# A state-space layer on one core: tokens on partitions for the norm, sums taken by ScalarE, and B replicated from fp32 rows

## The chip, the cores and the metric

The kernel runs on one core of a Trainium2 chip. A core has a matrix engine (PE, with its weight loads listed apart as PEld), a vector engine (DVE), a scalar engine (ACT), a general engine (POOL) and a sync engine (SP), which here issues all DMAs. Each runs its own list of instructions in order and waits for the others through semaphores. SBUF holds the working tiles, PSUM the outputs of PE. The metric is the device time in microseconds of one execution, and a time is the median of several runs.

## The reference

The network has four layers on x of shape (4, 96, 64, 64). The change lies in the first one alone: two Mamba blocks with residuals over sequences of 4096 tokens and 96 channels, a global pool, a 1x1 fusion and a batch norm over all tokens. Cut to what matters:

```python
def _mamba_block(seq, ...):                     # twice, for each of 4 batches
    mu = seq.mean(-1, keepdims=True)
    var = ((seq - mu) ** 2).mean(-1, keepdims=True)
    h = (seq - mu) * rsqrt(var + EPS) * ln_g + ln_b
    xs, z = split(h @ in_w)                     # 192 channels each
    xc = silu(causal_conv4(xs) + conv_b)
    dt, Bm, Cm = split(xc @ xproj_w)            # 6, 16, 16
    delta = softplus(dt @ dt_w + dt_b)
    dA = exp(delta[..., None] * A)              # 192 x 16 states
    dBx = delta[..., None] * Bm[:, :, None, :] * xc[..., None]
    hstates = scan(h = dA * h_prev + dBx)       # along the tokens
    y = einsum('blds,bls->bld', hstates, Cm) + Dp * xc
    return (y * silu(z)) @ out_w
...
out = fus_w @ concat([mamba_out, relu(pool(x) @ gp_w.T + gp_b)]) + fus_b
out = (out - out.mean((0, 2, 3))) * rsqrt(out.var((0, 2, 3)) + EPS) * bn_g + bn_b
return out + x
```

## The kernel before

Layer 0 cuts the 4096 tokens of a batch into 4 chunks of T = 1024. An item is one chunk of one batch in one of the two blocks, so there are 32 items, in the order chunk, block (i = 0 or 1), batch. The 192 x 16 = 3072 states of an item are 24 tiles of 128 partitions (32 channels times 4 states) by 1024 tokens.

For each tile m (24 to an item) the kernel does this:

- `rep` (from L191's helper `mm`, L195): PE multiplies a 0/1 matrix `sel_b` with rows that hold B, so that each of the four states' B is replicated over 32 partitions; the result `x` fills two banks of PSUM. One rep serves the tiles of a group (nine groups in an item, starting at tiles 0, 3, 6, 8, 11, 14, 16, 19 and 22).
- `exp` (L455): ACT computes dA as `exp(nega * delta)` from `ddb`, a copy of delta replicated through DRAM. For most tiles it goes to SBUF (`da`) three tiles ahead. For the eight tiles 2, 5, 7, 10, 13, 15, 18 and 21 it goes to PSUM (`dap`) one tile ahead, into the buffers that rep's `x` and `u` also use.
- `scan`: DVE multiplies `udb` (delta times xc, replicated) by rep's `x` into `u` in PSUM (L471), then scans (L475). For the eight tiles named above POOL has computed the product (`times_b`, L461, `up`), and DVE only scans.
- `times_c` (L481): POOL multiplies the states by C (`crep`); `sum_y` (L500): PE adds the states up into `y`; `gate` (L511): DVE multiplies by silu(z).

Everything else of an item is its first stage, spread over slots of tiles of the item before: a step marked `at_slot(t)` of item k is issued at tile 24 k + t - 24. Its steps are: load x (slot -11), `center` product that takes the mean off (-7), Square and a copy to `n` on ACT (-6), sum of squares by a product with ones (-5), Ln and Exp on ACT (-4), the scaling of `n` on DVE (-3, L299), the products with the conv taps `w_x` (-2 to 1), Silu, the product `xproj` that gives B, C (three times over) and dt (slot 5), and then delta and z. `project` (slot 39 of the item itself, 15 of the next) and `finish` (41) make the output `x`, and `keep_stats` (42, L537) takes batch statistics of it for i = 1.

B is replicated in bfloat16 as three parts that add up to the fp32 value: ACT casts the first 32 rows of the projection to `r3` (L335), PE subtracts that part from the other rows with the matrix `part` (`less`, L342), ACT casts again (`next_part`, L347), twice; rep then contracts over 96 rows.

`with tc.manual_schedule(...)` fixes the order on PE, DVE, ACT and POOL as it is written: within a tile, scan, rep or exp for the next tiles, times_c, keep_state, times_b, then the sums, project and finish, and last the first-stage steps of the items that follow. Only two one-bank buffers (`tile_ps`, tag `ps`) serve all first-stage products and project, so a step often waits for the eviction of an earlier one.

Of the kernel before, what the change touches and what calls it, by code (L numbers as in the profile page):

```python
# [50 lines left out]
class Net:  # L51
# [20 lines left out]
    def consts(self, ctx):  # L72
# [15 lines left out]
        self.stats = pool.tile([C, NT // MB, 6], F32, name="stats")  # L88
# [4 lines left out]
    def layer0(self, dram, scratch):  # L93
        tc, nc, ins = self.tc, self.nc, self.ins
        x_in = ins["x"]
        with ExitStack() as ctx:
# [19 lines left out]
            sel_b = cp.tile([C, 4, 128], BF16, name="sel_bq")  # L116
            part = cp.tile([C, 2, C], BF16, name="partq")
            fo = cp.tile([128, 3, C], F32, name="fo")
            dp = cp.tile([128, 2, 3, 128], F32, name="dp")
            sel_r = load(cp, "sel_r", [128, 32])  # L120
            xproj = load(cp, "xproj", [128, 3, 2, 3 * 2 * NST + DTR])
# [7 lines left out]
            fbias = cp.tile([C, B], F32, name="fbias")  # L129
            pooled = cp.tile([C, B * NSC], F32, name="pooled")  # L130

            with tc.tile_pool(name="l0s", bufs=1) as wk:
# [30 lines left out]
                nc.vector.tensor_copy(sel_b, load(wk, "sel_b", [C, 4, 128]))  # L163
                nc.vector.tensor_copy(part, load(wk, "part", [C, 2, C]))
# [14 lines left out]
            dbl = cp.tile([97 + DTR, T], F32, name="dbl")  # L179
            nc.vector.memset(dbl[C:], 1.0)  # L180
            r3s = [cp.tile([C, T], BF16, name=f"r3{k}") for k in range(2)]
            for r3 in r3s:
                nc.vector.memset(r3, 0.0)
# [7 lines left out]

            def mm(ps, w, rhs, start=True, stop=True, shift=0, **kw):
                for at in halves:
                    at_in = slice(at.start + shift, at.stop + shift)
                    nc.tensor.matmul(ps[:, at], w, rhs[:, at_in], start=start, stop=stop, **kw)  # L195
# [54 lines left out]
            def first_stage(k):  # L250
# [11 lines left out]
                @at_slot(-11)  # L262
                def _():
                    m["xn"] = load_x(b, s, i)
                    if s == 0:
                        nc.gpsimd.memset(n[:, :3], 0.0)
                    else:
                        nc.gpsimd.tensor_copy(n[:, :3], halo[:, b, i])

                @at_slot(-7)  # L270
                def _():
                    m["ps"] = [tile_ps(), tile_ps()]
                    for at, ps in zip(halves, m["ps"]):
                        nc.tensor.matmul(ps, self.center, m["xn"][:, at], start=True, stop=True)

                @at_slot(-6)
                def _():
                    m["sq"] = wk.tile([C, T], F32, name="sq", tag="sq")
                    for at, ps in zip(halves, m["ps"]):
                        nc.scalar.activation(m["sq"][:, at], ps, AF.Square)  # L280
                        nc.scalar.copy(n[:C, 3 + at.start : 3 + at.stop], ps)

                @at_slot(-5)
                def _():
                    m["ps"] = [tile_ps(), tile_ps()]
                    for at, ps in zip(halves, m["ps"]):
                        nc.tensor.matmul(ps, self.ones, m["sq"][:, at], start=True, stop=True)

                @at_slot(-4)
                def _():  # L290
                    for ps in m["ps"]:
                        nc.scalar.activation(ps, ps, AF.Ln, scale=1.0 / C, bias=self.eps[:C])
                        nc.scalar.activation(ps, ps, AF.Exp, scale=-0.5)

                @at_slot(-3)
                def _():
                    for at, ps in zip(halves, m["ps"]):
                        x = n[:C, 3 + at.start : 3 + at.stop]
                        nc.vector.tensor_mul(x, x, ps)  # L299
                    if s < NSC - 1:  # L300
                        nc.gpsimd.tensor_copy(halo[:, b, i], n[:, T:])
# [1120 lines left out]
```

## Time and profile before

| what | value |
|---|---|
| median of 6 runs | 4218.76 us (4212.11 to 4225.25) |
| the profiled execution | 4212.11 us, span 4210.3 us |
| PE busy | 3221.2 us, 77% of the span |
| DVE busy | 3189.2 us, 76% |
| POOL busy | 2997.1 us, 71% |
| ACT busy | 2513.9 us, 60% |
| mean granted clock of PE | 0.859 |
| layer 0 | from 0 to some 2725 us |

The profile is one execution, recorded by the hardware. A line of its groups gives the source line, the engine, the operation, the output and inputs by the program's names with their shapes, the count, the busy time in us and the mean of one instruction in ns, and then the idle time of that engine just before, with what ended it. A line of its timeline gives the start in us, the duration, the engine and the instruction; in brackets stands how long the engine was idle before and what released it. A line of its waits names who waited, for whom, how long in total, how often, and the longest. PEclk is the clock that was granted to PE as a share of full speed. An fp32 product appears as two records (and two weight loads), a bf16 product as one.

### The profile page before, as it was taken

The numbers are of one execution on the slowest core, as the hardware profiler recorded it, in microseconds if no ns is written. First come the engines' busy times: TensorE is split into PE (matmuls) and PEld (weight loads), VectorE is DVE, ScalarE is ACT, GpSimd is POOL, SyncE is SP. The second block draws the span as 40 slices with busy tenths as digits, with TensorE's granted clock in tenths as the row PEclk, the third lists the DMA queues.
The fourth block names the chain that finished last, engine by engine and source line by source line (L and its number), as shares of the span: only waits on it lengthen the run. The fifth ranks groups of instructions, "written<-read, shape, count | busy, mean of one in ns | idle before, by whom it ended". The sixth has DMA issues, their size and how long they took to land. (4 is left out here: it accounts for less than half of the span.)

```text
span 4210.3 us, 42511 instructions
## 1 busy us (share of the span) xinstructions
PE 3221.2 (77%) x13088; PEld 1305.3 (31%) x13088; DVE 3189.2 (76%) x2474; ACT 2513.9 (60%) x4098; POOL 2997.1 (71%) x1651
## 2 busy tenths in 40 slices
PE   6777677777767777776777776579999888888887
PEld 2112112111211111121112111177445436555642
DVE  4999999999999999999999999731222593433649
ACT  4666666666666666666666665222555575544547
POOL 1999999999999999999999999611120273433428
PEclk8888788888888887888888887669999998999989
DMA  6566566566656656565666556273000000001111
GB/s 171 137 157 165 137 152 162 137 148 157 166 134 151 158 145 148 151 166 131 152 161 151 143 146 167 70 226 131 0 0 1 1 1 6 24 26 28 44 46 53
DMA packets 183277, 468.02 MB, mean 111 GB/s; under 512 B 53108, under 2 KB 55134, under 8 KB 179968
## 3 DMA queue, kind: packets, MB, share of 16 engines
q1 hardware_dynamic: 183048, 465.31, 43.9%
q8 instruction: 103, 1.69, 0.2%
q14 instruction: 126, 1.03, 0.1%
HBM read 391.62 MB, written 73.50 MB: 110 GB/s over the span
## 5 line engine op out<-in xcount | busy, mean ns | idle before, releaser
L481 POOL TENSOR_TENSOR hs<-hs,crep 128x1024 f32<-128x1024 f32 x768 | 1798.5, 2358 | 111.3 <-DVE hs L475 60.8
L475 DVE TENSOR_TENSOR_SCAN hs<-da,state,u 128x1024 f32<-128x1024 f32 x384 | 901.8, 2348 | 24.8 <-DVE u L471 0.5
L455 ACT ACTIVATE dap<-ddb,nega 128x1024 f32<-128x1024 f32 x256 | 286.3, 1118 | 714.5 <-DVE u L471 708.3
L471 DVE TENSOR_TENSOR u<-udb,rep 128x1024 f32<-128x1024 f32 x512 | 627.7, 1226 | 75.8 <-PE rep L195 38.3
L455 ACT ACTIVATE da<-ddb,nega 128x1024 f32<-128x1024 f32 x512 | 583.8, 1144 | 68.0 <-DVE hs L475 66.1
L195 PE MATMUL rep<-r,sel_bq 96*128 96x512 bf16 x576 | 223.1, 478 | 504.8 <-DVE hs L475 495.6
L461 POOL TENSOR_TENSOR up<-udb,brep 128x1024 f32<-128x1024 f32 x256 | 604.7, 2362 | 5.2 <-DMA ud<-du 5.2
L500 PE MATMUL y<-hs,sel_r 128*32 128x512 f32 x3072 | 499.0, 720 | 4.7 <-POOL hs L481 4.7
L475 DVE TENSOR_TENSOR_SCAN hs<-dap,state,up 128x1024 f32<-128x1024 f32 x192 | 447.2, 2329 | 16.3 <-ACT dap L455 16.3
L205 PE MATMUL ps<-n,w_x 97*64 97x512 f32 x1536 | 435.5, 696 | 17.6 <-DVE n L299 17.5
L475 DVE TENSOR_TENSOR_SCAN hs<-da,u 128x1024 f32<-128x1024 f32 x128 | 293.0, 2289 | 8.0
L195 PEld LDWEIGHTS <-sel_bq 96*128 96x128 bf16 x576 | 38.6, 102 | 771.0 <-DVE hs L475 578.9
L1002 POOL CAST hq<-y 128x512 fp8e5<-128x512 f16 x192 | 117.9, 638 | 216.4 <-DVE y L1001 216.4
L205 PEld LDWEIGHTS ps<-n,w_x 97*64 97x64 f32 x1536 | 155.4, 158 | 296.7 <-issue 219.6
L205 PE MATMUL ps<-n,w_z 97*64 97x512 f32 x384 | 125.4, 738 | 133.1 <-ACT z L309 116.4
L1150 POOL TENSOR_TENSOR av<-av,ec 128x780 f32<-128x780 f32 x32 | 58.8, 1836 | 195.3 <-ACT av L1147 195.3
L796 POOL TENSOR_TENSOR xc<-xc,rs 96x512 f32<-96x512 f32 x32 | 40.4, 1264 | 208.0 <-ACT rs L795 198.2
L500 PEld LDWEIGHTS y<-hs,sel_r 128*32 128x32 f32 x3072 | 65.7, 116 | 322.5 <-issue 172.2
L219 PE MATMUL ps<-xc,xproj 64*102 64x512 f32 x384 | 150.5, 943 | 3.5 <-ACT xc L320 3.5
L475 DVE TENSOR_TENSOR_SCAN hs<-dap,up 128x1024 f32<-128x1024 f32 x64 | 145.2, 2269 | 7.6 <-ACT dap L455 4.7
L373 POOL TENSOR_TENSOR du<-delta,xc 128x512 f32<-128x512 f32 x96 | 122.1, 1272 | 31.9 <-ACT delta L357 22.2
L1147 ACT ACTIVATE av<-xr_ps,vec 128x65 f32<-128x65 f32 x384 | 116.8, 425 | 45.5 <-PE xr_ps L1135 45.5
(255 smaller groups left out, 6037.4 us busy)
## 6 DMA issues: line engine op xcount, KB each, us to landing
ddb<-dd SPq DMA_DIRECT2D x768, 128.0 KB, 3.4
udb<-ud SPq DMA_DIRECT2D x768, 128.0 KB, 4.4
crep<-cd SPq DMA_DIRECT2D x512, 128.0 KB, 4.0
brep<-cd SPq DMA_DIRECT2D x256, 128.0 KB, 3.8
dd<-delta SPq DMA_DIRECT2D x64, 384.0 KB, 3.9
ud<-du SPq DMA_DIRECT2D x192, 128.0 KB, 3.2
band<-in_band SPq DMA_DIRECT2D x24, 1024.0 KB, 4.8
gt<-in_idft SPq DMA_DIRECT2D x64, 256.0 KB, 2.7
```

What stands on the lines that cost most here:

```text
L195: nc.tensor.matmul(ps[:, at], w, rhs[:, at_in], start=start, stop=stop, **kw)
L205: nc.tensor.matmul(ps[rows], w[:, 64 * p : 64 * p + 64], rhs[:, at.start + shift : at.stop + shift], start=k == 0, stop=k == len(ws) - 1, ...
L219: nc.tensor.matmul(ps, w[rows, p], x[rows, p], start=start and p == 0, stop=p == 2)
L373: nc.gpsimd.tensor_mul(u, m["delta"][:, of], m["xc"][:, of])
L455: nc.scalar.activation(da, made[k]["dd", h, j], AF.Exp, scale=nega[:, col : col + 1])
L461: nc.gpsimd.tensor_mul(u, made[k]["ud", h, j], made[k]["brep", g])
L471: nc.vector.tensor_mul(u, made[k]["ud", h, j], x)
L475: nc.vector.tensor_tensor_scan(hs[:, 1:], made[k].pop(("da", t)), u, 0.0 if s == 0 else st, ALU.mult, ALU.add)
L481: nc.gpsimd.tensor_mul(hs[:, :T], hs[:, 1:], made[k]["crep", order[t][1]])
L500: nc.tensor.matmul(made[k]["y", p][row : row + 32], sel_r, made[k]["hs", t][:, at], start=False, stop=True, skip_group_check=True,)
L1002: nc.gpsimd.tensor_copy(q[:, m, :], y2, saturate=False)
L1147: nc.scalar.activation(v[:, k, d], xr[:, at], AF.Identity, scale=self.v128(w, cg + d), bias=self.v128(bias, cg + d))
```

## The change

Three things change in layer 0.

- The norm. The centre product now takes x as the stationary operand, 128 tokens at a time, so that tokens lie on partitions: eight products into two banks. ACT squares each piece of 96 columns and takes its sum in the same instruction (`accum_out`), then Ln and Exp on a [128, 8] tile, then scales each piece with its own column (`nc.scalar.mul`). Eight products with the identity turn the pieces back, and ACT copies them into `n`. DVE's scaling is gone. The halo copies move from POOL to ACT; POOL keeps a memset for the first chunk.
- The batch statistics. `finish` lets ACT's eviction take the sum, and a second ACT instruction on the same bank squares the shifted value and takes its sum. `keep_stats` is gone, and `bn_aggr` becomes two reductions and four small steps on DVE.
- B. The three bfloat16 parts are gone, with their casts and the `part` products. rep multiplies fp32 rows of `dbl`: rows 0 to 31 for the first 512 tokens, rows 32 to 63 for the second. `dbl` gets a second buffer. The steps after it move up: delta from slots 10 to 12 to slots 7 to 10, Softplus from 12 to 10, z from 12 to 14 to 10 to 13, the store of delta from 13 to 11, and Silu of z from 19 to 16.

```diff
-        self.stats = pool.tile([C, NT // MB, 6], F32, name="stats")
+        self.sums = pool.tile([C, NT // MB], F32, name="sums")
+        self.squares = pool.tile([C, NT // MB], F32, name="squares")
+        self.shift = pool.tile([C, 1], F32, name="shift")
...
                 @at_slot(-11)
                 def _():
                     m["xn"] = load_x(b, s, i)
-                    if s == 0:
-                        nc.gpsimd.memset(n[:, :3], 0.0)
-                    else:
-                        nc.gpsimd.tensor_copy(n[:, :3], halo[:, b, i])
                 @at_slot(-7)
                 def _():
-                    m["ps"] = [tile_ps(), tile_ps()]
-                    for at, ps in zip(halves, m["ps"]):
-                        nc.tensor.matmul(ps, self.center, m["xn"][:, at], start=True, stop=True)
+                    m["ps"] = [tile_ps(128), tile_ps(128)]
+                    for q in range(8):
+                        nc.tensor.matmul(
+                            m["ps"][q // 4][:, q % 4 * C : q % 4 * C + C],
+                            m["xn"][:, q * 128 : q * 128 + 128],
+                            self.center,
+                            start=True,
+                            stop=True,
+                        )
                 @at_slot(-6)
                 def _():
-                    m["sq"] = wk.tile([C, T], F32, name="sq", tag="sq")
-                    for at, ps in zip(halves, m["ps"]):
-                        nc.scalar.activation(m["sq"][:, at], ps, AF.Square)
-                        nc.scalar.copy(n[:C, 3 + at.start : 3 + at.stop], ps)
+                    m["nt"] = wk.tile([128, 8, C], F32, name="nt", tag="nt")
+                    m["rs"] = wk.tile([128, 8], F32, name="rs", tag="rs")
+                    for q in range(8):
+                        nc.scalar.activation(
+                            m["nt"][:, q],
+                            m["ps"][q // 4][:, q % 4 * C : q % 4 * C + C],
+                            AF.Square,
+                            accum_out=m["rs"][:, q : q + 1],
+                        )
+                    nc.scalar.activation(m["rs"], m["rs"], AF.Ln, scale=1.0 / C, bias=self.eps)
+                    nc.scalar.activation(m["rs"], m["rs"], AF.Exp, scale=-0.5)
                 @at_slot(-5)
                 def _():
-                    m["ps"] = [tile_ps(), tile_ps()]
-                    for at, ps in zip(halves, m["ps"]):
-                        nc.tensor.matmul(ps, self.ones, m["sq"][:, at], start=True, stop=True)
+                    for q in range(8):
+                        x = m["ps"][q // 4][:, q % 4 * C : q % 4 * C + C]
+                        nc.scalar.mul(m["nt"][:, q], x, m["rs"][:, q : q + 1])
                 @at_slot(-4)
                 def _():
-                    for ps in m["ps"]:
-                        nc.scalar.activation(ps, ps, AF.Ln, scale=1.0 / C, bias=self.eps[:C])
-                        nc.scalar.activation(ps, ps, AF.Exp, scale=-0.5)
+                    m["ps"] = [tile_ps(), tile_ps()]
+                    for q in range(8):
+                        nc.tensor.matmul(
+                            m["ps"][q // 4][:, q % 4 * 128 : q % 4 * 128 + 128],
+                            m["nt"][:, q], self.ident, start=True, stop=True)
                 @at_slot(-3)
                 def _():
+                    if s == 0:
+                        nc.gpsimd.memset(n[:, :3], 0.0)
+                    else:
+                        nc.scalar.copy(n[:, :3], halo[:, b, i])
                     for at, ps in zip(halves, m["ps"]):
-                        x = n[:C, 3 + at.start : 3 + at.stop]
-                        nc.vector.tensor_mul(x, x, ps)
+                        nc.scalar.copy(n[:C, 3 + at.start : 3 + at.stop], ps)
                     if s < NSC - 1:
-                        nc.gpsimd.tensor_copy(halo[:, b, i], n[:, T:])
+                        nc.scalar.copy(halo[:, b, i], n[:, T:])
...
                     for at, ps in zip(halves, m["ps"]):
-                        nc.scalar.copy(r3[:32, at], ps[:32])
                         nc.scalar.copy(dbl[:nb, at], ps[:nb])
...
-                for r in range(2):
-                    at_slot(7 + 2 * r)(lambda r=r: less(r))
-                    at_slot(8 + 2 * r)(lambda r=r: next_part(r))
-                parts_of("delta", [(dtw[:, i], 0)], dbl, ((10, 11), (10, 12), (11, 12)), 1)
-                @at_slot(12)
+                parts_of("delta", [(dtw[:, i], 0)], dbl, ((7, 8), (7, 9), (9, 10)), 1)
+                @at_slot(10)
                 def _():
                     nc.scalar.activation(m["delta"], m["delta"], AF.Softplus)
                     exp_set()
-                parts_of("z", [(w_z[:, i], 3)], n, ((12, 13), (13, 14), (13, 14)), 3)
+                parts_of("z", [(w_z[:, i], 3)], n, ((10, 11), (11, 12), (12, 13)), 3)
...
                 x = psum_x.tile([128, T], F32, name="rep", tag="xu")
-                mm(x, sel_b[:, order[t][1], :], made[k]["r3"])
+                for q, at in enumerate(halves):
+                    rows = slice(32 * q, 32 * q + 32)
+                    nc.tensor.matmul(
+                        x[:, at], sel_b[rows, order[t][1]], made[k]["dbl"][rows, at], start=True, stop=True
+                    )
...
-                    else:
-                        nc.scalar.activation(o[:, at], ps, AF.Identity, bias=fbias[:, b : b + 1])
+                        continue
+                    a = (b * L + s * T + at.start) // MB
+                    nc.scalar.activation(
+                        o[:, at], ps, AF.Identity, bias=fbias[:, b : b + 1], accum_out=self.sums[:, a : a + 1]
+                    )
+                    if (b, s, at.start) == (0, 0, 0):
+                        nc.vector.tensor_scalar_mul(self.shift, self.sums[:, :1], 1.0 / MB)
+                        nc.vector.tensor_scalar(sbias, fbias, self.shift, None, ALU.subtract)
+                    nc.scalar.activation(
+                        ps, ps, AF.Square, bias=sbias[:, b : b + 1], accum_out=self.squares[:, a : a + 1]
+                    )
...
-                        if at == 42 and items[k0][2]:
-                            keep_stats(k0)
```

## The prediction

> **What bounds the kernel now.** First the page's slices, because shares over the whole span mix layers.
>
> ```profile
> DVE  4999999999999999999999999731222593433649
> ACT  4666666666666666666666665222555575544547
> POOL 1999999999999999999999999611120273433428
> ```
>
> Layer 0 fills slices 1 to 25, and there DVE and POOL are both full. Which of the two leads is told by the busy times of a stretch of it and by the waits of each (200 to 2700 us, 30.5 items).
>
> ```profile
> core 0: us, PE busy (x) PEld busy (x) DVE busy (x) ACT busy (x) POOL busy (x), PEclk, DMA share, GB/s
> 1000.00:1500.00 500.00, 360.62 (x1402) 94.80 (x1404) 477.17 (x282) 328.21 (x509) 475.04 (x226) 0.84 0.60 149
> ```
>
> ```profile
> DVE u L471 <- PE rep L195: 31.8, 38, 1.5
> DVE hs L475 <- ACT dap L455: 20.1, 27, 0.9
> DVE u L471 <- DMA ud<-du: 11.6, 9, 1.4
> DVE hs L475 <- POOL hs L481: 2.8, 3, 0.9
> ```
>
> ```profile
> POOL hs L481 <- DVE hs L475: 55.5, 45, 2.3
> POOL halo L301 <- DVE n L299: 17.4, 21, 1.0
> ```
>
> POOL waits for DVE, DVE hardly for POOL: DVE sets the pace. One item of 24 tiles takes 82.0 us (the scan of tile 15 of the first item starts at 135.73 us, that of the thirty-first at 2596.44: 2460.7 / 30). POOL's own floor is near below: back to back its 128x1024 products start every 2.33 us (6.99 for three), so 24 + 8 of them and three of 1.26 make 78.4 us.
>
> Where DVE waits I took from its timeline, item by item; this is one item, with the work around it.
>
> ```profile
> 1034.13 2.35 DVE L475 TENSOR_TENSOR_SCAN hs<-dap,state,up 128x1024 f32<-128x1024 f32 x1 [0.77 <-ACT dap L455]
> 1037.30 1.23 DVE L471 TENSOR_TENSOR u<-udb,rep 128x1024 f32<-128x1024 f32 x1 [0.82 <-DMA ud<-du]
> ...
> 1044.45 1.05 ACT L527 COPY x<-ps 96x512 f32<-96x512 f32 x2
> 1044.55 2.32 DVE L475 TENSOR_TENSOR_SCAN hs<-dap,state,up 128x1024 f32<-128x1024 f32 x1
> ...
> 1045.08 1.96 PE L274 MATMUL ps<-x,center 96*96 96x512 f32 x4 [2.35 <-ACT x L527]
> ...
> 1046.87 0.60 PE L195 MATMUL rep<-r,sel_bq 96*128 96x512 bf16 x2
> ...
> 1047.50 1.23 DVE L471 TENSOR_TENSOR u<-udb,rep 128x1024 f32<-128x1024 f32 x1 [0.63 <-PE rep L195]
> ```
>
> Three places return in nearly every item: tile 15 (23.9 us in 31 items, ACT late after the Softplus of slot 12), tile 16 (34.5 us; the rep for it ran at 1036.54 to 1037.26, so the DMA named is not the true releaser), and tile 19 (10.6 us in 17 items, rep queued on PE behind the centre products of slot 17). That is 0.77 + 1.11 + 0.34 = 2.2 us an item.
>
> **The change part by part.** DVE loses two instructions in each item and two more in each second-layer item:
>
> ```profile
> L299 DVE TENSOR_TENSOR n<-n,ps 96x512 f32<-96x512 f32 x58 | 37.6, 668 | 0.8 <-ACT ps L293 0.6
> L537 DVE BATCH_NORM_STATS2 stats<-x 96x6 f32<-96x512 f32 x30 | 18.8, 668 | 0.0
> ```
>
> 37.6 / 29 = 1.30 us, and 18.8 / 15 = 1.25 us in every second item, 0.63 on average: 1.93 us an item off the leading engine. POOL loses its halo copies (0.19 us each) and the wait of 17.4 / 21 = 0.83 us before one of them; it follows DVE, so this only lowers its floor.
>
> The row for 96x512 on DVE is 0.67 us, and the same scaling comes back on ACT as eight pieces, in an engine 66% busy. The Trainium skill (ScalarE: Activation LUTs, Rules for kernel authors) speaks against that: multiplications belong on VectorE. Followed, it would keep the 1.30 us on DVE; the waits above say that here DVE's time is the dearer.
>
> ACT's new work: 512-column copies start every 0.48 us and last 0.57, a one-column copy lasts 0.17 and lets the next start after 0.08. From these an immediate-scale piece of 96 columns starts about every 0.15 us (estimate: 0.08 + 96 x 0.40 / 511), one with a scale read from a tile about 0.1 more (673 against 574 ns where a bias is read). No row shows an accumulated sum: between 0 and 0.2 us each (a one-column write as an instruction of its own, 0.17); I take 0.08, nearest to how such copies overlap. Eight Squares and eight scalings are then 3.9 us, Ln and Exp 0.5, the copies into n and the halo 1.2, against four evictions of 0.48, two Ln of 0.67 and two Exp of 0.49 removed (4.2 us), and six bf16 casts (2.9). What counts is dap of tile 21, which stands behind the scalings. It can't start before u 20 has ended, some 12.5 us after u 17 (four scans, two products, a gate, and tile 19's wait). In a second-layer item ACT reaches it 10.6 us after u 17: 2.9 to finish's first copy, 3.2 until centre's second half is done, then four squares 0.9, Ln and Exp 0.5, da 22 1.05, scalings 2.0. That leaves 1.9; twelve sums at 0.2 would take 1.4 of it. So nothing, and every microsecond beyond would be paid in full.
>
> Softplus moves from slot 12 to 10, and Silu of z from 19 to 16, into 4.9 us that ACT idles before dap 18 (they need 4.05). Around slot 10 ACT has 9.5 us of work (four exps, two copies, Softplus with its two table loads 4.05) in the 12.5 between u 9 and the end of scan 12, and nothing else at slot 12. z's copies no longer stand behind Softplus with PE blocked in front of rep 16 (109 us of PE waits for z). I take the waits of tiles 15 and 16 as gone: -1.88. On SP the dd stores move ahead of the load of x and wait for an earlier Softplus: nothing. B's three-part chain (casts, four 0.38 us products) had no waiter on DVE: nothing.
>
> PE: rep becomes two fp32 products in row groups 0 and 1, two records each. Do they run side by side? The nearest rows are the projections with 64-row groups: twelve records take 2.69 us at clock 1.0, 0.22 each, where a full-height fp32 record takes 0.43 (1.96 us for four, less the 0.2 in which the last one drains). So yes by that row: 2 x 0.43 + 0.2 = 1.06 us warm (four paired z records: 1.08), 1.9 at half clock, against 0.60 and 1.03. rep may start when the scan before last is done and is needed one scan (2.33 us) later: it still fits wherever PE is free. It isn't free at tile 19. The centre products become 16 small records: 0.13 each by L892 (97x97, 33.8 us / 256), 0.22 by the same shape in L714 at half clock (55.2 / 256).
>
> Let F be the end of finish's first copy, when centre starts; DVE could start u 19 at F + 1.8. First-layer items: centre 2.1, rep 1.06: F + 3.2, a wait of 1.4. Second-layer items: finish's two 0.67 us evictions become four with sums, the second bank comes free at F + 2.1, half of centre is 1.05, rep 1.08: F + 4.2, a wait of 2.4. Mean 1.9, and 0.4 for a rep at half clock in half of the items, since project, no longer held by a late rep 16, ends earlier and PE then idles some 3.3 us before centre: 2.3 against 0.34, +2.0. In this trace centre stayed warm after 2.35 us of idling, while the w_x products after 1055 us ran at 0.57 after gaps of 3.1 and 1.2. By the skill's rule (TensorE: Matmul & The Clock Gate, Part 1), one idle window of some 3.4 us halves the clock; that would make it the second rival's +31 us.
>
> Tiles 0 and 8: rep 0 ended 0.34 us before it was needed, rep 8 1.16; both now end 0.5 to 1.3 later: +0.4 together. Transposes (16 records, 2.2 to 3.1 us) stand in front of rep 22 but begin some 4 us earlier: nothing. Around the loop: the first item loses the 2.5 us of casts and gains about as much in norm; at the end, squares and the small DVE steps (0.16 each) replace an aggregate of 1.02: 0, give or take 3.
>
> Sum: -1.93 - 1.88 + 2.0 + 0.4 = -1.4 us an item, 31 times: -44. The profiled execution took 4212.1 us (span 4210.3 and 1.8 around it), 6.7 under the median of the six runs, 4218.8. So 4168 for it, 4175 as a median.
>
> **The rivals.** (1) Tile 19's wait doesn't grow, because centre starts earlier or the pieces overlap. Then -3.5 an item until POOL's 78.4 us binds: -109, 4110; half of it 4144. For it: POOL idles 5% and would have to be caught up. Against: in-order PE with rep behind centre.
> (2) Slower: PE runs at half clock from slot 17 on. Centre 3.5, rep 1.9 give a wait of 3.6, in second-layer items (sums at 0.2) 4.5; tiles 0 and 8 cost 1.1. Then -3.81 + 3.7 + 1.1 = +1.0 an item, +31: 4250. It decides once the new waits exceed 3.8 us an item. For it: the longer gap before centre; against: centre at clock 1.0 now.
> (3) The row groups don't run side by side: rep is 1.9 us warm, 3.6 at half clock (36% of the reps by their mean of 477 ns between 390 and 635). 9 x 0.36 x (3.6 - 2.33) = 4.1, and 0.85 more at tiles 0, 8 and 19: +6.7 - 1.4, +164: 4340. Against it is the projections' rate.
>
> **How the numbers follow.** Forecast 0.52, its own range 4150 to 4205; (1) 0.20, (2) 0.20, (3) 0.08. Runs of this kernel tell 0.2%, 8.4 us, from nothing. Faster: 0.46 + 0.20 = 0.66; same: 0.06 + 0.04 = 0.10; slower: 0.16 + 0.08 = 0.24. The range 4128 to 4250 leaves out (3), the lower part of (1) (0.06) and what of (2) lies above (0.05).
>
> **What would show it.** Right: no DVE waits at tiles 15 and 16, one of 1.4 to 3 us at tile 19 behind rep, rep records in overlapping pairs near 1.06 us, an item of 80.6 us. Wrong: an item under 79.5 with POOL never idle; rep over 1.9 us at clock 1.0; waits for dap 18 or 21; waits for POOL's up.

## The result, and the profile after

The changed kernel takes 4229.92 us (median of 19 runs, 4224.33 to 4238.48) against 4219.37 for the kernel before in the same session (41 runs). The ratio is 1.0025, with a 95% interval of 1.0017 to 1.0033: slower by some 10.5 us, where 44 us less was forecast. The profiled execution took 4231.81 us, 4230.0 of it span.

The slices of the changed kernel's page; layer 0 still fills slices 1 to 25, with DVE and POOL both near full:

```profile
DVE  4999999999999999999999999731222583434649
ACT  4666666666666666666666565322555575544547
POOL 2999989999999999999999999711120274333418
```

The same 500 us of layer 0 as before (busy time and records of PE, PEld, DVE, ACT, POOL, then granted clock, DMA share, GB/s):

```profile
1000.00:1500.00 500.00, 409.82 (x1629) 113.78 (x1621) 461.00 (x260) 324.47 (x627) 471.02 (x213) 0.80 0.61 149
```

DVE is busy for 461 us where it was 477, PE for 410 where it was 361, and the clock is 0.80 where it was 0.84. DVE has less to do and more to wait for. Its waits between 200 and 2700 us (us in total, times, longest) say for whom:

```profile
DVE u L473 <- PE rep L442: 120.8, 92, 4.5
DVE u L473 <- DMA ddb<-dd: 6.1, 12, 0.8
```

Before, rep was named for 31.8 us and dap for 20.1. Dap is gone from the list, and rep's share has almost quadrupled.

Where these waits lie can be added up by tile from the traces, as a mean over the 30 items from the first scan of the second item to that of the last (us an item; "clock 0.5" is the share of that time in which PE had half its clock):

| kernel | item | DVE busy | waits over 0.15 us | of which at tiles | clock 0.5 |
|---|---|---|---|---|---|
| before | 82.07 | 78.00 | 2.32 | 15: 0.77, 16: 1.13, 19: 0.35 | 0.34 |
| changed | 82.59 | 76.46 | 4.33 | 0: 0.31, 3: 0.23, 8: 0.94, 14: 0.57, 19: 2.24 | 0.39 |

The two old waits went as forecast. Waits at tiles 0, 3, 8 and 14 came, and tile 19's grew. This is tile 8 in the changed kernel's timeline (start, duration, engine):

```profile
1090.41 2.08 PE L442 MATMUL rep<-dbl,sel_b 32*128 32x512 f32 x4 [5.45 <-DVE hs L477]
1092.42 4.83 PE L212 MATMUL ps<-xc,xproj 64*102 64x512 f32 x12
1097.18 1.07 PE L502 MATMUL y<-hs,sel_r 128*32 128x512 f32 x8
1098.18 1.13 PE L442 MATMUL rep<-dbl,sel_b 32*128 32x512 f32 x4
1099.35 1.23 DVE L473 TENSOR_TENSOR u<-udb,rep 128x1024 f32<-128x1024 f32 x1 [0.89 <-PE rep L442]
```

PE idles for 5.45 us, then runs rep 6 at half clock (2.08 us), then twelve projections of slot 5, of which the first ones run at half clock too, then y, and only then rep 8. DVE stands 0.89 us. The kernel before ran the same chain with the shorter rep:

```profile
1001.72 1.03 PE L195 MATMUL rep<-r,sel_bq 96*128 96x512 bf16 x2 [6.25 <-DVE hs L475]
1002.68 4.50 PE L219 MATMUL ps<-xc,xproj 64*102 64x512 f32 x12
1007.11 1.06 PE L500 MATMUL y<-hs,sel_r 128*32 128x512 f32 x8
1008.11 0.60 PE L195 MATMUL rep<-r,sel_bq 96*128 96x512 bf16 x2
1009.95 1.23 DVE L471 TENSOR_TENSOR u<-udb,rep 128x1024 f32<-128x1024 f32 x1
```

Rep 6 was at half clock there too (1.03 us where rep 8 takes 0.60), but rep 8 was done 1.2 us before u 8 began. At tile 14 of the changed kernel it is the same picture as at tile 8: rep 11 comes after 3.6 us of idling and takes 2.08 us, and y (1.94 us), two parts of z (1.98 each) and y's product with `dp` (2.08), all at half clock, follow in front of rep 14.

At tile 19 it matters what the kernel before did there behind a second-layer item, one of the second block (i = 1); its finish, and the wait for it, fall into tiles 17 to 19 of the item that follows, which is meant where a second-layer item is said to wait. This is its timeline:

```profile
1209.00 1.96 PE L274 MATMUL ps<-x,center 96*96 96x512 f32 x4 [2.45 <-ACT x L529]
1210.61 1.25 DVE L537 BATCH_NORM_STATS2 stats<-x 96x6 f32<-96x512 f32 x2
1210.80 0.59 PE L195 MATMUL rep<-r,sel_bq 96*128 96x512 bf16 x2
1211.79 1.21 DVE L471 TENSOR_TENSOR u<-udb,rep 128x1024 f32<-128x1024 f32 x1
```

The two bn_stats ran while rep 19 was being made. Rep 19 ended at 1211.39 and u 19 began at 1211.79, so of their 1.25 us only some 0.4 cost anything. In the changed kernel the same place reads:

```profile
1214.83 0.68 ACT L533 ACTIVATE x<-ps,fbias 96x512 f32<-96x512 f32 x1
1215.50 0.63 ACT L539 ACTIVATE ps<-ps,sbias 96x512 f32<-96x512 f32 x1
1216.16 0.67 ACT L533 ACTIVATE x<-ps,fbias 96x512 f32<-96x512 f32 x1
...
1217.65 1.13 PE L264 MATMUL ps<-center,x 96*128 96x96 f32 x8 [0.20 <-ACT ps L539]
1218.71 1.46 PE L442 MATMUL rep<-dbl,sel_b 32*128 32x512 f32 x4
1220.20 1.23 DVE L473 TENSOR_TENSOR u<-udb,rep 128x1024 f32<-128x1024 f32 x1 [2.95 <-PE rep L442]
```

The Square of the first half stands between the two evictions, the second half of centre waits for the second Square, and rep 19 for centre. DVE waits 2.95 us here, and 2.5 to 3.4 in the other second-layer items (4.5 in one that is shown next); in first-layer items it waits 1.3, but 2.5 in the first four.

One item stands out in the trace: the sixth takes 89.5 us from first scan to first scan, its neighbours 81.9 and 81.7. In it lies the only pair of DVE instructions that makes shift and sbias:

```profile
552.42 0.15 DVE L537 TENSOR_SCALAR shift<-sums 96x1 f32<-96x1 f32 x1 [1.44 <-ACT x L533]
552.60 4.71 DVE L538 TENSOR_SCALAR sbias<-fbias,shift 96x4 f32<-96x4 f32 x1
552.65 2.34 POOL L483 TENSOR_TENSOR hs<-hs,crep 128x1024 f32<-128x1024 f32 x1
554.95 2.34 POOL L463 TENSOR_TENSOR up<-udb,brep 128x1024 f32<-128x1024 f32 x1
557.35 0.65 ACT L539 ACTIVATE ps<-ps,sbias 96x512 f32<-96x512 f32 x1 [4.96 <-DVE sbias L538]
```

A step of 96x4 elements takes 4.71 us and ends, at 557.31, where two POOL products in a row have ended. ACT, centre and rep 19 wait behind it. The Trainium skill (SBUF — State Buffer, SBUF: two separate sides) says that a pair of ports is shared by GpSimd and a VectorE step that runs in a two-port mode or reads two inputs from SBUF, that whichever starts first holds it for its whole instruction, and that the other blocks meanwhile. The end of the step at the end of a POOL product fits that. Whether this step is of that kind, and why it waited out two products, no run here shows, nor does any separate the port from another tie to POOL.

### The profile page after: what moved, and what is told of

Same layout as the page of the kernel before. It is cut to its first block, busy times and chain, and to the rows that moved or that the text cites. A ratio compares the mean times of both kernels' runs of the same rounds, so it can differ in the third digit from the quotient of the medians.

```text
span 4230.0 us, 45622 instructions
## 1 busy us (share of the span) xinstructions
PE 3468.1 (82%) x14304; PEld 1424.2 (34%) x14304; DVE 3134.1 (74%) x2382; ACT 2484.2 (59%) x4690; POOL 2993.2 (71%) x1603
## 5 line engine op out<-in xcount | busy, mean ns | idle before, releaser
L442 PE MATMUL rep<-dbl,sel_b 32*128 32x512 f32 x1152 | 435.2, 838 | 485.5 <-DVE hs L477 475.2
L502 PE MATMUL y<-hs,sel_r 128*32 128x512 f32 x3072 | 489.0, 710 | 4.5 <-POOL hs L483 4.5
L198 PE MATMUL ps<-n,w_x 97*64 97x512 f32 x1536 | 397.6, 664 | 2.5 <-POOL n L307 2.5
L442 PEld LDWEIGHTS rep<-dbl,sel_b 32*128 32x128 f32 x1152 | 106.8, 222 | 698.5 <-issue 359.7
L198 PEld LDWEIGHTS ps<-n,w_x 97*64 97x64 f32 x1536 | 114.6, 152 | 297.1 <-issue 253.8
L198 PE MATMUL ps<-n,w_z 97*64 97x512 f32 x384 | 151.3, 880 | 3.6 <-ACT z L321 3.6
```

What stands on the lines that cost most here:

```text
L198: nc.tensor.matmul(ps[rows], w[:, 64 * p : 64 * p + 64], rhs[:, at.start + shift : at.stop + shift], start=k == 0, stop=k == len(ws) - 1, ...
L442: nc.tensor.matmul(x[:, at], sel_b[rows, order[t][1]], made[k]["dbl"][rows, at], start=True, stop=True)
L502: nc.tensor.matmul(made[k]["y", p][row : row + 32], sel_r, made[k]["hs", t][:, at], start=False, stop=True, skip_group_check=True,)
```

## The experiments

The parts are: the **norm** (tokens on partitions), the **sums** (batch statistics on ACT), the **rep** (fp32 products from two row groups), and the **slots** (Softplus, delta, z and Silu earlier), which came with the rep. Each kernel was timed beside the kernel before, whose median was 4219 to 4223 us in these sessions.

Three theories stood at the start. A: an item is DVE's work plus its waits for rep, and the long fp32 rep, half the time at half clock, brought the new waits. B: POOL's work or the transfers hold the item at 82 us. C: the grid on which PE's clock changes holds it there.

**One part at a time.** `norm_only` is the kernel before with the norm:

```diff
-    nc.vector.tensor_mul(x, x, ps)                          # slot -3
+    nc.scalar.mul(m["nt"][:, q], x, m["rs"][:, q : q + 1])   # slot -5, eight pieces
```

> The kernel before with the new norm alone; B's three bfloat16 parts, the slots of Softplus, z and Silu, and bn_stats stay. Theory A (the time is DVE's work plus its waits for rep, and the change's loss comes from the longer fp32 rep): DVE loses the two multiplications, 1.30 us an item, rep keeps its 0.60 us, tiles 15 and 16 keep their waits of 0.75 and 1.08, tile 19 gains at most 0.3 (centre 2.1 against 1.96): -1.0 an item, 31 times, about 4188 (4178 to 4198). Theory B (POOL's work or the transfers hold an item at 82 whatever DVE does): 4219, with the 1.3 us back as waits for POOL or a DMA. Theory C (PE's clock, which in the traces changes only on a grid of 3.413 us, holds an item at 24 grid steps, 81.92 us, as long as some of its reps run at half clock): about 4219 too, but with the 1.3 us back as waits for rep and most items between 81.8 and 82.0.

Measured: 4252.05 us, ratio 1.0069 (1.0057 to 1.0082): slower, which none of the theories had. Its waits, 200 to 2600 us, show a place that none had named:

```profile
DVE hs L494 <- ACT dap L474: 67.2, 58, 1.8
```

Tile 21 waits 1.50 us an item for dap. Silu of z still stands at slot 19, in front of the scalings, and dap 21 behind both. The prediction's sum for dap 21 leaned on Silu moving to slot 16 in the same change (`slots_norm` below has both, and no wait at 21). The gain on DVE was 0.96, not 1.30.

`stats_only` is the kernel before with the sums:

```diff
-    nc.scalar.activation(o[:, at], ps, AF.Identity, bias=...)
+    nc.scalar.activation(o[:, at], ps, AF.Identity, bias=..., accum_out=self.sums[...])
+    nc.scalar.activation(ps, ps, AF.Square, bias=..., accum_out=self.squares[...])
-    if at == 42 and items[k0][2]: keep_stats(k0)
```

> The kernel before with the batch statistics as ScalarE's sums alone. Theory A: DVE loses bn_stats, 0.63 us an item on average; finish of a second-layer item becomes four evictions with sums, so tile 19 waits about 1.2 us more in every second item (0.6 on average): 0 an item; the one DVE step that makes sbias waits out POOL's product as in the changed kernel, 4 to 8 us once. Together 4222 to 4230. If that one step costs nothing here: 4219. Theories B and C: 4219 plus the same one-off.

Measured: 4253.90 us, ratio 1.0077 (1.0065 to 1.0089). Tile 19 waits 2.5 to 3.8 us in second-layer items and still 0.5 to 0.8 in most first-layer ones, 1.76 on average against 0.35; the step of sbias took 4.32 us here and its item 88.9. The one-off was there as expected, the price at tile 19 was more than twice what I had put down.

`b_only` is the kernel before with rep and slots:

```diff
-    mm(x, sel_b[:, order[t][1], :], made[k]["r3"])
+    nc.tensor.matmul(x[:, at], sel_b[rows, order[t][1]], made[k]["dbl"][rows, at], ...)  # rows 0-31, 32-63
```

> The kernel before with B replicated by fp32 products and Softplus, z and Silu in their new slots; norm and bn_stats stay on DVE. Theory A: the waits at tiles 15 and 16 go (-1.83 us an item), rep of 1.13 us warm and 2.08 at half clock adds waits at tiles 8, 14, 0 and 19 (+0.89, +0.56, +0.26 and about +0.7): +0.6 an item, about 4237 (4215 to 4245). Theory B: 4219. Theory C: the item stays at 81.9 unless DVE's work and waits pass it: 4219 to 4225. If instead rep's length costs nothing, the waits at 15 and 16 are a plain gain: 4219 - 57 = 4162.

Measured: 4207.87 us, ratio 0.9964 (0.9952 to 0.9976). The waits at 15 and 16 went (-1.90), those at 8 (0.64), 14 (0.71), 0 (0.21) and 19 (0.78) came: 2.39 against 2.32. My 4237 took tiles 8 and 19 for dearer than they were, by 0.25 and 0.27 an item.

`after_shift_act` is the changed kernel with

```diff
-    nc.vector.tensor_scalar_mul(self.shift, self.sums[:, :1], 1.0 / MB)
-    nc.vector.tensor_scalar(sbias, fbias, self.shift, None, ALU.subtract)
+    nc.scalar.mul(self.shift, self.sums[:, :1], -1.0 / MB)
+    nc.scalar.activation(sbias, fbias, AF.Identity, bias=self.shift)
```

> The changed kernel with the shift and sbias of the first half computed on ScalarE in place of VectorE; nothing else differs. If the one period of 89.5 us (item 5, against 81.9 around it) comes from the one DVE step of 4.71 us that ended only as POOL's products changed over: 4230 - 7.6 = 4222, and no period over 85. If that period has another cause (the accumulated sum read back, the table, the transfers): 4230.

Measured: 4223.04 us, ratio 1.0000 (0.9991 to 1.0010), and the sixth item takes 83.0 us. So the one step on DVE was worth 6.5 us by that item and 7 by the medians, and without it the whole change is no change.

**Undoing a part of the change.** `norm_b` is the changed kernel without the sums (the diff of `stats_only`, reversed):

> The changed kernel with bn_stats on VectorE in place of ScalarE's sums; the new norm, the fp32 rep and the new slots stay. Theory A2, formed after the first four runs (bn_stats runs in the time in which VectorE waits for rep 19 of the following item anyway, and the sums make finish longer, so centre and rep 19 come later): the step of sbias, 7 us, goes, and in each of the 15 items behind a second-layer item a wait of 2.95 us at tile 19 becomes bn_stats of 1.25 with a wait of at most 0.5 behind it, -1.2 to -1.7: 4230 - 7 - 22 = 4201, and with what tile 3 waited (0.2 an item) 4195. Theory C (items held at 24 steps of PE's clock grid): items of 81.9 both ways, 4212. The prediction's own reading (bn_stats' 0.63 us an item is saved in full): 4230 - 7 + 19 - 20 = 4222.

Measured: 4202.32 us, ratio 0.9957 (0.9939 to 0.9974), as theory A2 had it; second-layer items wait 0.3 us at tile 19 (1.3 in the first). A second-layer item in its timeline:

```profile
1202.73 1.26 DVE L536 BATCH_NORM_STATS2 stats<-x 96x6 f32<-96x512 f32 x2
1203.08 1.13 PE L439 MATMUL rep<-dbl,sel_b 32*128 32x512 f32 x4
1204.25 1.23 DVE L470 TENSOR_TENSOR u<-udb,rep 128x1024 f32<-128x1024 f32 x1 [0.27 <-PE rep L439]
```

Bn_stats lies in the wait for rep 19 again, and 0.27 us of it are left.

`after_sq_late` keeps the sums and changes the order in finish:

```diff
     for at, ps in zip(halves, made[k]["out"]):
         nc.scalar.activation(o[:, at], ps, AF.Identity, bias=..., accum_out=...)
-        nc.scalar.activation(ps, ps, AF.Square, bias=sbias[:, b : b + 1], accum_out=...)
+    for at in halves:
+        nc.scalar.activation(sq, o[:, at], AF.Square, bias=self.shift, accum_out=...)
```

> The changed kernel with finish in another order: both evictions with their sums first, then the two Squares, which read the evicted half out of SBUF with the shift as bias (sbias is not needed, and the shift is computed on ScalarE). Theory A2: both PSUM banks come free 1.4 us earlier for centre's second half, so the wait at tile 19 in items behind a second-layer item falls from 2.95 to about 1.6: -1.35 x 15 - 7 for the step of sbias = 4203, if the Squares, now later on ScalarE, don't make dap 21 late (they have 1.9 us by the prediction's sum). If the wait at tile 19 is PE's half clock and not the order: 4223.

Measured: 4206.32 us, ratio 0.9970 (0.9958 to 0.9981), with 1.4 to 1.5 us at tile 19 in second-layer items in place of 2.5 to 3.4 (2.0 to 2.5 in the first four), and nothing at tile 21. Apart from the step of sbias, the Squares between the evictions were most of the price of the sums. Without them u 19 starts 3.3 us behind the end of finish's first eviction, as in `norm_b` (3.2): a wait of 1.5 has taken the place of bn_stats and its 0.3.

`after_warm` keeps PE busy with products of zeros:

```diff
+    if m >= 0 and t + 1 in {6: 20, 11: 12, 16: 8, 22: 8}:
+        for _ in range(n):   # zeros, added into the open y bank
+            nc.tensor.matmul(made[k]["y", p], zero_w, zero_x, start=False, stop=True, ...)
     xu = rep(m + 1)
```

> The changed kernel with shift and sbias on ScalarE, and with bfloat16 products of zeros, added into open y banks, in PE's idle time before reps 6, 11, 16 and 22 (20, 12, 8 and 8 of 512 columns), so that PE has no idle stretch of over 3 us there. Theory A (reps 6 and 11 run at half clock after idle stretches of 5.4 and 3.6 us, and what PE does until slots 8 and 14 is late by that): the granted clock rises, rep 6 and 11 take 1.1 instead of 2.1 us, the waits at tiles 8 and 14 go (-1.5 an item): 4223 - 47 = 4176. Less where the zeros themselves delay a rep: by up to 0.4 us at four tiles, 4176 to 4210. If the waits at tiles 8 and 14 come from the number of records and not from the clock: 4223 or more.

Measured: 4229.54 us, ratio 1.0027 (1.0015 to 1.0039), nothing gained, though the clock rose from 0.842 to 0.896 and the waits at 0, 8 and 14 went. Its timeline shows who took the gain:

```profile
1126.44 3.73 PE L268 MATMUL ps<-center,x 96*128 96x96 f32 x16 [3.29 <-ACT x L539]
1130.10 2.08 PE L446 MATMUL rep<-dbl,sel_b 32*128 32x512 f32 x4
1132.22 1.23 DVE L477 TENSOR_TENSOR u<-udb,rep 128x1024 f32<-128x1024 f32 x1 [3.98 <-PE rep L446]
```

Project ended sooner, PE idled 3.29 us before centre, and now centre (3.73 against 2.03 us) and rep 19 ran at half clock: tile 19 went from 2.22 to 3.92 an item. The prediction's second rival, centre and rep 19 at half clock, is this state, and at its price (3.6 to 4.5).

**Clock against length.** `norm_b_warm2` and `sq_late_warm2` add twelve more such products before centre, to `norm_b` and to `after_sq_late` (there the Squares' unused output is bfloat16); `norm_b_pad` adds one bn_stats whose output is not used; `after_rep_bf16` makes rep from one bfloat16 rounding of B, leaves out its two lower parts, and has one `dbl` again:

```diff
+    keep_warm(k - 2, 1, 12)                                  # slot -7, before centre
...
+    nc.vector.bn_stats(extra, m["xn"][:, :MB])               # norm_b_pad, slot 3
...
-    nc.tensor.matmul(x[:, at], sel_b[rows, ...], made[k]["dbl"][rows, at], ...)
+    nc.tensor.matmul(x[:, at], sel_b16[rows, ...], made[k]["r1"][rows, at], ...)   # after_rep_bf16
```

> The kernel of norm_b (new norm, fp32 rep, new slots, bn_stats) with bfloat16 products of zeros, added into open y banks, in PE's idle time before reps 6, 11, 16 and 22 (20, 12, 8 and 8) and before centre (12); the last place is new against after_warm, where the clock rose from 0.842 to 0.896, the waits at tiles 0, 8 and 14 went, and centre ran at half clock instead, so that tile 19 took it all back. Theory C2 (each half-clock stretch of PE moves the loss to whichever rep falls into it, and items settle at 24 steps of the 3.413 us grid; without half-clock stretches the item is DVE's 76.8 and its short waits): the waits at 0, 8 and 14 go (-1.96 an item), tile 19 stays near 1.0: item 79.8, 4202 - 60 = 4142. Theory B (POOL's 77.7 us of work with its hand-overs, or the transfers, hold the item): 4190 to 4205 with waits for POOL or a DMA in place of rep.

Measured: 4164.01 us, ratio 0.9871 (0.9856 to 0.9885); clock 0.923, item 80.38. The waits at 8 and 14 are gone, tile 19 stays at 0.94, and of 60 us expected 38 came; tiles 0 and 3 keep 0.5 between them.

> The kernel of after_sq_late (the whole change, Squares behind both evictions) with the same products of zeros before reps 6, 11, 16 and 22 and before centre. Theory C2: waits at 0, 8 and 14 go (-2.0 an item), tile 19 falls from 1.44 to about 1.1: 4206 - 62 - 10 = 4134 to 4144. Theory B: 4190 to 4210.

Measured: 4170.15 us, ratio 0.9885 (0.9867 to 0.9902); tile 19 stays at 1.62. Even with Squares last and PE warm, the sums gain nothing over bn_stats.

> The kernel of norm_b with one more bn_stats of 96x512 on VectorE in each item (0.67 us, at slot 3 of the item, where VectorE doesn't wait; its output is not used). Theory A (an item is VectorE's work plus the waits that PE's queue gives it): +0.67 x 31 = +21, 4223. Theory C (from the ninth item on, items stand at 81.9 with the scan of tile 0 always at the same place of PE's clock grid, while items 6 to 8 took 80.0 to 80.2; the waits at tiles 8, 14, 19 and 0 take up what VectorE gains or loses, until it has lost 1.7): the locked items stay at 81.9 and the waits fall by 0.67: 4202 to 4208.

Measured: 4209.81 us, ratio 0.9979 (0.9969 to 0.9988): 7.5 us more than `norm_b`, for 21 us more work on DVE. DVE's busy time rose by 0.58 an item and the waits fell by 0.33. Nearer to theory C than to A: from the thirteenth item on the items stand at 81.9 in both kernels; the 7.5 us came in the items before.

> The changed kernel with shift and sbias on ScalarE, and rep made from one bfloat16 rounding of B in the same row groups: it leaves out the two lower parts of B. Rep is then 0.3 to 0.6 us at either clock against 1.13 warm and 2.08 at half clock; ScalarE gets two casts of 0.4 us more an item. Theory A: the waits at tiles 0, 3, 8 and 14 go (-1.9 an item) and tile 19's falls by 0.6: -2.5 x 31 from 4223: 4146. Theory B (POOL's 77.7 us of work and its hand-overs): the gain stops where POOL binds, about 79.5 an item, 4138. Theory C (grid): items stay at 81.9: 4205 to 4215.

Measured: 4153.11 us, ratio 0.9842 (0.9827 to 0.9857), 70 us below `after_shift_act`. Waits at 3, 8 and 14 are gone, tile 0 keeps 0.31, tile 19 falls from 2.22 to 1.44, the item from 82.47 to 80.07, while the clock stays where it was (0.848). What DVE waits for, in `after_rep_bf16` and then in `norm_b_warm2`, 200 to 2600 us:

```profile
DVE u L476 <- PE rep L445: 49.1, 32, 3.8
```

```profile
DVE u L476 <- PE rep L445: 42.6, 40, 2.9
```

At tiles 8 and 14 a short rep at half clock and a long rep on a warm PE come to the same: it is the two together, rep at 2.08 us, that DVE feels. Theory C, that the clock's grid holds an item at 81.9 as long as some reps run at half clock, falls as the cause: `after_rep_bf16` spends as much of its time at half clock as `after_shift_act` (0.38 and 0.39), and its items take 80.1. So does B: POOL and the transfers have the same work in both kernels as in the changed one, and the items are 80.1 and 80.4.

**The early slots with the old rep.** `slots_only` keeps the three bfloat16 parts and draws their chain together:

```diff
-    at_slot(7 + 2 * r)(lambda r=r: less(r))
-    at_slot(8 + 2 * r)(lambda r=r: next_part(r))
+    at_slot(7 + r)(lambda r=r: less(r))
+    at_slot(7 + r)(lambda r=r: next_part(r))
-    parts_of("delta", ..., ((10, 11), (10, 12), (11, 12)), 1)   # Softplus 12, z 12-14, Silu 19
+    parts_of("delta", ..., ((8, 9), (8, 10), (10, 11)), 1)      # Softplus 11, z 11-14, Silu 16
```

> The kernel before with its three bfloat16 parts of B, but with the chain of parts in slots 7 and 8 instead of 7 to 10, delta in slots 8 to 10, Softplus at 11, z in 11 to 13 and Silu at 16: about the slots of the changed kernel, with the short rep. If the waits that the changed kernel has at tiles 8, 14 and 0 come from the length of the fp32 rep: the waits at tiles 15 and 16 (1.83 an item) go and nothing comes in their place, 4219 - 57 = 4162; Softplus stands one slot later than in the changed kernel, so up to 0.7 of tile 15's wait may stay (4184). If they come from the crowding of delta, z and y in slots 7 to 13: as b_only, 4208.

Measured: 4180.55 us, ratio 0.9899 (0.9883 to 0.9915). No waits at 15 and 16, none at 8 or 14, and next to none at 0. With `after_rep_bf16`, which has the slots of the changed kernel to the letter, this shows that the waits at 8 and 14 come from rep's length and not from the slots. For tile 0 it isn't shown: `slots_norm`, next, has the short rep and 0.30 there. Tile 19 has 0.66 and tile 13 0.13.

`slots_norm` adds the norm to it, and `slots_norm_warm` the products of zeros as well.

> The kernel of slots_only with the new norm too; bn_stats and the three bfloat16 parts stay. Against norm_only (4252) the waits at tile 21 (1.43), 15 and 16 (1.95) go: 4252 - 105 = 4147. Against norm_b (4202) it differs by rep and one slot of Softplus: if the fp32 rep is what costs, 4202 - 1.96 x 31 = 4141. If the slots cost it: about 4200.

Measured: 4160.43 us, ratio 0.9852 (0.9836 to 0.9867), between the two expectations and near the first; the wait at tile 21 is gone. Its rep waits, 200 to 2600 us:

```profile
DVE u L490 <- PE rep L195: 23.3, 23, 1.8
```

> The kernel of slots_norm with the products of zeros before reps 6, 11, 16 and 22 and before centre. If the clock matters only through the length of rep and of centre before rep 19: rep of 0.6 or 1.03 us fits anyway, and at most 0.3 to 0.5 us an item is left to gain: 4130 to 4147. If the zeros delay short reps: up to 4160.

Measured: 4152.69 us, ratio 0.9836 (0.9822 to 0.9851). With a short rep the half clock is worth some 8 us (the two intervals overlap), with the long one it was worth 38 (`norm_b` to `norm_b_warm2`). This kernel computes all of the reference and is the fastest of those that do, 1.6% under the kernel before.

## Why the prediction was wrong, by its own steps

The last runs take the change apart into a chain of kernels, each with one part more. The prediction's sum falls into the same parts: the slots are its -1.88; the norm -1.30 and 0.14 for centre; the rep 0.46 at tile 19, 0.4 for half clock, 0.4 at tiles 0 and 8; the sums -0.63 and what is left of tile 19's +2.0, 1.0.

| part added | from, to | forecast, an item x 31 | measured (medians) |
|---|---|---|---|
| slots | before, `slots_only` | -1.88: -58 | -41 |
| norm | `slots_only`, `slots_norm` | -1.16: -36 | -20 |
| fp32 rep | `slots_norm`, `norm_b` | +1.26: +39 | +42 |
| sums | `norm_b`, changed | +0.37: +11 | +28, of it 7 once |

The measured column sums to +8 and, with 2 us by which the kernel before differed between sessions, to the +10.5 of the result. Parts taken in another order weigh differently: the norm alone costs 30 us in the old slots. And `slots_only` has Softplus one slot later than the change.

In the two traces the sum misses by 1.8 us an item, with the step of sbias left out (+0.4 where -1.4 was forecast), and 1.65 of it lies in one term, that of tiles 0 and 8.

**Waits at 15 and 16 (-1.88).** Right: gone in every kernel with the early slots. But in `slots_only` 0.5 of it came back at once, 0.31 at tile 19, 0.13 at 13 and 0.10 in gaps under 0.15 us: what the chain of tile 16 no longer held, the next one did.

**DVE's -1.93.** Mis-sized: the busy time fell by 1.71 (76.29 against 78.00, with the step of sbias taken out). The sum added durations of 0.67 us, but such records overlap: in the changed kernel's timeline one of 0.67 lets the next start after 0.58 (z at 1086.01, u at 1086.59), and in the trace before the removed ones let the next start after 0.59 on average, which makes 1.78. Start to start is nearer to what an instruction frees; the last 0.07 is not explained.

**Tile 19 (+2.0).** Right in sum, 2.24 for a forecast of 2.3, and right in its chain: the second half of centre starts 2.1 us after the end of finish's first eviction in second-layer items, as forecast, and rep 19 at 3.2. Most first-layer items wait 1.3, as forecast without half clock (1.4); the first four wait 2.5, because there DVE is done with scan 18 some 0.9 us earlier against finish and centre starts 0.26 later, which no step foresaw. Second-layer items wait 2.5 to 3.4 for a forecast of 2.4: in ten of thirteen rep 19 runs wholly or in part at half clock and takes 1.4 to 2.1 us in place of 1.13, for which the forecast had 0.4 as a mean. That the sum came so near is in part luck. What the step didn't ask is whether the price was worth paying: `norm_b` has 0.3 us of wait there with bn_stats inside, so the sums took 1.25 us of work off DVE in a second-layer item and put 2.2 to 3.1 us of waiting in its place.

**Tiles 0 and 8 (+0.4), and nothing at 3 and 14.** This is the step that failed: 2.05 us an item at tiles 0, 3, 8 and 14. It sized each rep's lateness by that rep alone. At tile 8 two reps and the projections between them are in the chain: rep 6 at half clock is 1.05 us longer than a bfloat16 one at half clock, xproj takes 4.89 where it took 4.65 (medians), rep 8 is 0.53 longer, 1.8 us in all. The step put 0.5 to 1.3 of lateness against the 1.16 of slack that it read in one item; the mean slack in the trace before is 0.91, so 0.9 is missing, and 0.94 was measured. At 14 it is rep 11, then y and two parts of z on a cold PE, moved there by the early slots. At tiles 8 and 14 `after_rep_bf16`, `slots_only` and `norm_b_warm2` have no waits. What makes those at 0 and 3, 0.54 together, stays open: `after_rep_bf16` keeps 0.31 at tile 0 and `norm_b_warm2` 0.25 and 0.29 at tiles 0 and 3, but in a few items of 1.3 to 3.3 us each, where the changed kernel waits 0.2 to 0.8 us at tile 0 in most items.

**Around the loop (0).** The first scan comes 1.9 us earlier, and from the last scan to the last step of the batch norm's scale and shift it takes 1.3 us less: within the forecast's 3. But the "small DVE steps (0.16 each)" held one of 4.71 us with three engines behind it, 7 us in all. The two profiled executions differ by 19.7 us, more than the medians: 15.1 lie in the items, and the stretch behind the last scan, 1502 and 1509 us here, ranges from 1498 to 1514 over the traces of all kernels.

**The rivals.** (3), row groups one after the other, is false: rep takes 1.13 us warm and 2.08 cold, the paired rate. (1) didn't come: tile 19 grew, and even the short rep of `after_rep_bf16` leaves 1.44 there. (2) named the right cause, the half clock, and put it at the wrong place: in the changed kernel centre is warm in most items, and the cold reps that DVE feels are 6 and 11, which were cold in the kernel before too. It comes true in `after_warm`. The rule cited from the Trainium skill (TensorE: Matmul & The Clock Gate, Part 1), that an idle window of about 3.4 us halves the clock, agrees with the idle 5.45 and 3.6 us before those two reps. It doesn't cover the drops behind windows in which PE was partly busy (last section).

The rule of the Trainium skill against the norm (ScalarE: Activation LUTs, Rules for kernel authors: multiplications belong on VectorE) gives the right choice in the old slots, where the norm on ScalarE costs 30 us (by the wait for dap 21 behind Silu and the scalings), and not in the early ones, where it gains 20.

## What to carry to other kernels

Before taking work off the leading engine, look in its timeline for what runs beside that work: an instruction that lies in a wait costs little or nothing, and removing it buys as little, least of all if its replacement stands in the chain that ends the wait. Size a lengthened step on an in-order engine over the whole chain up to the next consumer, at the clock that the trace shows at each record, not at the consumer's own record alone. When several parts come in one change, forecast and run them apart: here two of four gained 61 us, and the other two lost 70.

## What the runs showed of the hardware

- The accumulated sum of an ACT instruction is read by a second instruction, 216 ns long behind pieces of 96 columns and 193 to 196 behind 512.
- Two fp32 products of 32 rows in row groups 0 and 1 run side by side: their records start in pairs, and the four take 1.13 us warm, 2.08 at half clock, where four full-height records (centre before) took 1.96 warm.
- PE's granted clock changes on a grid of 3.413 us. In the changed kernel, between 200 and 2600 us, it stayed at 1.0 only after windows of that grid in which PE was busy for at least 0.54, fell after windows with a median of 0.2 (0 to 0.85), and rose again only after windows that were full, by the ends that the profile models for products. So by these records no fully idle window is needed.
- In several kernels the items settle at 81.9 us, 24 steps of that grid (81.92): in `norm_b` from the tenth item on, with the scan of tile 0 always within 0.2 us of the same phase and half-clock stretches beginning at the same four places of the item in 22 to 28 of 29 items. That waits take up what DVE's work changes is what `norm_b_pad` shows; why these phases hold an item, and whether they would hold another kernel's, is open.
- A DVE step of 96x4 elements took 4.71 and 4.32 us beside POOL's products. With the same step on ACT that item of the changed kernel took 83.0 us in place of 89.5.
